# Spreading copies and norms between ScalarE, VectorE and GpSimd in a four-stage transformer block

## The chip, the cores and the metric

The kernel runs on one core of one Trainium2 chip. A core has five engines that run their own instruction streams and meet through semaphores: TensorE (PE in the profile, with its weight loads as PEld), VectorE (DVE), ScalarE (ACT), GpSimd (POOL) and SyncE (SP), which here only issues transfers. The metric is the device time of one execution in microseconds (us); shorter is better. The time of a kernel is the median of its runs.

## The reference

The input `x` is 8 batches of 128 tokens with 128 features, in float32. Eight sublayers are applied, each as `x = x + f(layernorm(x))`: four pairs of a cross attention over a context of 77 tokens and a feed-forward part. This change touches the third pair (called L2) and everything after it:

```python
x = x + _L1_ffn_ref(...)      # 64 experts, three per token: rows of y are gathered and weighed
x = x + _L2_xattn_ref(_layernorm(x), ctx, ...)   # rotary, 16 heads of 8, norms after, ReLU feed-forward
x = x + _L2_ffn_ref(_layernorm(x), ...)          # 6 local attention layers, window 32, 16 heads of 64
x = x + _L3_xattn_ref(_layernorm(x), ctx, ...)   # 8 heads of 64
x = x + _L3_ffn_ref(_layernorm(x), ...)          # 2 local attention layers, window 64, 8 heads of 64

# one local layer, h = features 64..127 taken from the token before
q, k, v = split(shift(x) @ Wqkv)
q, k = rotate(l2norm(q) * qs), rotate(l2norm(k) * ks)
x = x + local_attention(q, k, v) @ Wo
h = layernorm(shift(x)) * g + b
a, gate = split(h @ W1 + b1)
x = x + (a * gelu(gate)) @ W2 + b2
```

`_L2_xattn_ref` itself normalises twice: `x = layernorm(query + o)`, then `layernorm(x + relu(x @ W1) @ W2)`.

## The kernel before, in words

The activations stay on the chip: one batch is 128 partitions (tokens) by 128 features. Nearly all matmuls are in float32.

**How the order is made.** A layer doesn't issue instructions. It adds *steps* to a `Plan` (line 537): what a step reads and writes, and a nominal cost in ns on each engine that may run it, such as `{"ACT": 490, "DVE": 450}`. `arranged` (line 606) then plays the whole plan through with these costs: whenever an engine is free it takes the ready step of lowest rank, and a step with two engines goes to the one that comes to it first. The result is a fixed order per engine and a fixed choice of engine for each step. A changed cost, or a second engine for a step, can therefore reorder everything behind it, on PE too. There are two plans: "front" (up to the experts) and "later" (from L2's cross attention on). Once built, each engine runs its own list strictly in that order.

**The gather stage.** `plan_later` takes the batches two by two. For one batch, `one` (line 1586) has GpSimd issue three indirect transfers (`gathered`, line 1504) that fetch the rows of the experts' result; VectorE weighs and adds them to `x` (line 1517). Then comes the norm (`normed` and `scaled`, lines 772 and 778): VectorE finds mean and variance (lines 783, 785); GpSimd adds epsilon (776), takes the power -1/2 (790), negates the mean (791) and multiplies it by the root (792); ScalarE writes the normalised rows with that scale and bias (800), or VectorE does with mean and root alone (802). In this plan `norms_on_act` is set, so it is always ScalarE. The rows are transposed on PE (762), copied out of PSUM (749 on ScalarE, 751 on VectorE), projected twice, multiplied by the rotary tables (1549), and the two halves are added on GpSimd (1553). `attend_8` follows: scores (855), exponentials (863), sums and outputs (871), a reciprocal (877) and, only as a watch on overflow, two additions on GpSimd (881, 882). `layer` (line 1603) then takes two batches through norm, affine (1650), feed-forward with ReLU (1620 or 1622), and a second norm.

**The local layers.** They work on halves of four batches. `shifted` (line 1833) transposes `y` on PE and copies it out of PSUM as two pieces of 64 partitions, the second one token later. `queries_keys` (line 1851) does for each batch, for queries and keys and each group of eight heads: a projection (1847), squares on ScalarE (1868), two rotary products and a sum on VectorE (1869, 1871, 1873), an addition on GpSimd (1874), the inverse length (1899 to 1907), a product on GpSimd (1887), four transposes and a copy out of PSUM. `attention` follows (1952, 1958: band and scores; 1965: exponentials; 2013 and 2019, or 1992 and 1998: sums and outputs; 1973 to 1981: division; 1933: projection). `gated` (line 2028) is the feed-forward part; its step `gates` (2058, 2059) is one block on ScalarE: load the table for Gelu, three Gelus, load the table for exponentials back.

PE runs its matmuls in tile modes: whole, quarters, columns and so on; the plan charges a change of mode with 100 ns.

Of the kernel before, what the change touches and what calls it, by code (L numbers as in the profile page):

```python
# [19 lines left out]
ALU = mybir.AluOpType  # L20
# [4 lines left out]
P = 128  # L25
B = 8
KC = 77
EPS = 1e-5
# [676 lines left out]
class Work:  # L705
# [63 lines left out]
        self.plan.add({"PE": ns}, lambda e: nc.tensor.matmul(out(), lhsT=lhsT(), rhs=rhs(), start=start, stop=stop),  # L769
                      reads, writes, "full", opens)  # L770

    def normed(self, outs, ins, reads, writes, a=1.0, b=EPS, n=4):


        self.scaled(outs, ins, reads, writes,
                    lambda nc, t, v: nc.gpsimd.tensor_scalar(t, v, float(a), float(b), ALU.mult, ALU.add), n)

    def scaled(self, outs, ins, reads, writes, under, n=4):
        c, nc, plan = self.c, self.c.nc, self.plan
        st, mv, va, nb = self.tile([P, n, 6]), self.tile([P, n, 2]), self.tile([P, 2 * n]), self.tile([P, n])  # L780
        for k in range(n):
            one = reads if len(reads) != n else [reads[k]]
            plan.add({"DVE": 282}, lambda e, k=k: nc.vector.bn_stats(st()[:, k, :], ins(k)), one, [st])
        for k in range(n):
            plan.add({"DVE": 158}, lambda e, k=k: nc.vector.bn_aggr(mv()[:, k, :], st()[:, k, :]), [st], [mv])
        scale = lambda k: va()[:, n + k : n + k + 1]

        def root(e):
            under(nc, va()[:, 0:n], mv()[:, 0:n, 1])
            nc.gpsimd.tensor_tensor(va()[:, n : 2 * n], va()[:, 0:n], c.mhalf[:, 0:n], ALU.pow)  # L790
            nc.gpsimd.tensor_scalar(nb(), mv()[:, 0:n, 0], -1.0, None, ALU.mult)
            nc.gpsimd.tensor_tensor(nb(), nb(), va()[:, n : 2 * n], ALU.mult)

        plan.add({"POOL": 930 + 150 * n}, root, [mv], [va, nb])
        for k in range(n):
            one = reads if len(reads) != n else [reads[k]]

            def scaled(e, k=k):
                if e == "ACT":
                    nc.scalar.activation(outs(k), ins(k), AF.Identity, bias=nb()[:, k : k + 1], scale=scale(k))  # L800
                else:
                    nc.vector.tensor_scalar(outs(k), ins(k), mv()[:, k, 0:1], scale(k), ALU.subtract, ALU.mult)

            plan.add({"ACT": 490} if self.norms_on_act else {"ACT": 490, "DVE": 450}, scaled,
                     [*one, mv, va, nb], writes if len(writes) != n else [writes[k]])

    def softmax(self, sc, n, by_head=False):

# [29 lines left out]
    def attend_8(self, qT, at, kb, vz, j, wo, bias, mask=None, qv=None):  # L838
# [5 lines left out]
        c, nc, plan = self.c, self.c.nc, self.plan  # L844
# [21 lines left out]
        cl, rs, oT = self.tile([P, P]), self.tile([P, P]), self.tile([P, P])  # L866
# [11 lines left out]
        plan.add({"DVE": 282}, lambda e: nc.vector.tensor_tensor(oT(), av(), rs(), ALU.mult), [av, rs], [oT])  # L878

        def watch(e):  # L880
            nc.gpsimd.tensor_tensor(cl(), cl(), rs(), ALU.add)
            nc.gpsimd.tensor_tensor(c.total, c.total, cl(), ALU.add)

        plan.add({"POOL": 650}, watch, [rs, self.total], [cl, self.total])
        return self.projected_8(oT, wo, bias)

    def projected_8(self, oT, wo, bias):
# [359 lines left out]
class Routed:  # L1247
# [256 lines left out]
    def gathered(self, w, b):  # L1504

        c, nc, plan = w.c, w.c.nc, w.plan
        x = w.xs[b]
        for k in range(TOPK):
            g = w.tile([P, P])

            def get(e, k=k, g=g):
                self.got[b] = nc.gpsimd.indirect_dma_start(
                    out=g()[:, :], out_offset=None, in_=self.ys[:, :],
                    in_offset=bass.IndirectOffsetOnAxis(ap=self.srci[:, b, k : k + 1], axis=0)).ins

            plan.add({"POOL": 1000}, get, [w.landed], [g], tail=2300)
            plan.add({"DVE": 382}, lambda e, k=k, g=g: nc.vector.scalar_tensor_tensor(
                x(), g(), self.gate[:, b, k : k + 1], x(), ALU.mult, ALU.add), [g, x], [x])


class Context:
# [18 lines left out]
    def rotated(self, out, src, reads, name, which, m, n):  # L1540

        w = self.w
        c, nc, plan = w.c, w.c.nc, w.plan
        t = []
        for k, wname in enumerate((name, name + "_pair")):
            ps, tt = w.bank([P, m, n]), w.tile([P, m, n])
            w.mm(lambda ps=ps: ps().rearrange("p b s -> p (b s)"), lambda wname=wname: c.get("w", "L2_W" + wname), src,
                 reads, [ps], 1.7 * max(n * m, 130), opens=[tt])
            plan.add({"DVE": 200 + 1.1 * n * m}, lambda e, ps=ps, tt=tt, wname=wname, k=k: nc.vector.scalar_tensor_tensor(
                tt(), ps(), c.get("col", "L2_b" + wname), spread(self.rope[:, 2 * which + k, 0:n], m, 1), ALU.add, ALU.mult),  # L1550
                [ps], [tt])
            t.append(tt)
        plan.add({"POOL": 240 + 2.0 * n * m}, lambda e: nc.gpsimd.tensor_tensor(
            out() if m > 1 else out().unsqueeze(1), t[0](), t[1](), ALU.add), t, [out])

    def keys(self, h):
# [24 lines left out]
def plan_l2_xattn(w, ctx, route):  # L1581
# [4 lines left out]
    def one(b):  # L1586

        x, (xh, xT, qT, y) = w.xs[b], (w.tile([P, P]) for _ in range(4))
        route.gathered(w, b)
        w.normed(lambda k: xh(), lambda k: x(), [x], [xh], n=1)  # L1590
        tp = w.turn(lambda k: xh(), [xh], n=1)
        w.copy(xT, lambda: tp()[:, 0, :], [tp], [xT], 294, 290)
        ctx.rotated(qT, xT, [xT], "q", 0, 1, P)
        if b >= 4:
            ctx.values(b)
        out = w.attend_8(lambda: qT().unsqueeze(1), 0, ctx.kbs[b // 4], ctx.vzs[b % 4], b % 4, c.get("w", "L2_Wo"),
                         c.get("row", "L2_xattn_bo"), qv=qT)
        plan.add({"DVE": 282}, lambda e: nc.vector.tensor_tensor(y(), xh(), out(), ALU.add), [xh, out], [y])
        ys[b] = y
# [3 lines left out]
    def layer(b0, n):  # L1603
        xs, y = w.xs[b0 : b0 + n], [ys[b0 + j] for j in range(n)]
        y1 = w.tile([P, n, P])
        w.normed(lambda k, y1=y1: y1()[:, k, :], lambda k, y=y: y[k](), y, [y1], n=n)
        affine(w, y1, "L2_xattn_g1", "L2_xattn_b1", n)
        yT = w.tile([P, n, P])
        tp = w.turn(lambda k, y1=y1: y1()[:, k, :], [y1], n=n)
# [26 lines left out]
        plan.add({"DVE": 145 + 134 * n}, lambda e, y1=y1, y2=y2, out=out: nc.vector.tensor_tensor(y2(), y1(), out(), ALU.add),  # L1636
                 [y1, out], [y2])
        y3 = w.tile([P, n, P])
        w.normed(lambda k, y3=y3: y3()[:, k, :], lambda k, y2=y2: y2()[:, k, :], [y2], [y3], n=n)
        affine(w, y3, "L2_xattn_g2", "L2_xattn_b2", n)  # L1640
        xv = c.x[:, b0 : b0 + n, :]
        plan.add({"POOL": 80 + 300 * n}, lambda e, y3=y3, xv=xv: nc.gpsimd.tensor_tensor(xv, xv, y3(), ALU.add), [y3, *xs], xs)
# [115 lines left out]
class Local:  # L1758
# [74 lines left out]
    def shifted(self, b0, n):  # L1833

        nc, plan = self.c.nc, self.plan
        hs = self.tile([P, n, P])
        y = self.y
        tp = self.turn(lambda k: y[:, b0 + k, :], self.ys[b0 : b0 + n], n=n)
        plan.add({"POOL": 150}, lambda e: nc.gpsimd.memset(hs()[64:128, :, 0:1], 0.0), [], [hs])
        self.copy(lambda: hs()[0:64], lambda: tp()[0:64], [tp], [hs], 180 + 103 * n)  # L1840
        self.copy(lambda: hs()[64:128, :, 1:P], lambda: tp()[64:128, :, 0 : P - 1], [tp], [hs], 180 + 103 * n)
        return hs

    def projected(self, layer, hs, j, o, opens):
# [6 lines left out]
    def queries_keys(self, layer, hs, j):  # L1851
# [33 lines left out]
        for i in range(2 * ng):  # L1885
# [2 lines left out]
                t(), t1(), spread(r()[:, 8 * i : 8 * i + 8], 64, 2), ALU.mult), [t1, r], [t])  # L1888
            tp = self.turn(lambda k, t=t: t().rearrange("p h d -> p (h d)")[:, k * P : (k + 1) * P], [t])
            qT = self.tile([P, 4, P])  # L1890
            self.copy(qT, tp, [tp], [qT])
            out.append(qT)
        return out[:ng], out[ng:]

# [398 lines left out]
```

## Time and profile before

| what | value |
| --- | --- |
| median of three runs | 1497.15 us (1496.13 to 1500.06) |
| the profiled execution | 1488.41 us, its span 1486.4 us |
| PE busy, share of the span | 1389.6 us, 93% |
| VectorE, ScalarE, GpSimd busy | 918.6, 918.3, 825.9 us |
| mean granted TensorE clock | 0.977 of full speed |
| copies out of PSUM on ScalarE (749) | 519, mean 561 ns |
| copies out of PSUM on VectorE (751) | 73, mean 643 ns |

Times in a profile are those of one execution; it was 8.7 us shorter than the median. The span runs from the first to the last instruction. The stages by time: front and experts to about 374 us, gathers and L2's cross attention mixed with the first local layers to about 525 us, the six local layers of L2 to about 1200 us, L3 to the end. A busy PE in the profile is one with a matmul in flight; "idle before" is the time that an engine stood still just before an instruction.

### The profile page before, as it was taken

Reading aid. Unit: us, or ns where it says so; the run is one execution under the profiler, and the core shown is the slowest. Engines: PE = TensorE matmul, PEld = TensorE weight load, DVE = VectorE, ACT = ScalarE, POOL = GpSimd, SP = SyncE. Lnnn points to the kernel's source line nnn. Section 1 sums busy time; section 2 is a strip of 40 time slices with the busy share of each in tenths; the row PEclk is TensorE's granted clock in tenths of the full one; section 3 lists DMA queues with packets and bytes.
Section 4 is the critical chain, followed back from the end, with each engine's and each line's share of the span. In section 5 each row is a group of like instructions: output and inputs, shape, how many; then the busy total and the mean of one; then the engine's idle time right before and its main releaser. Section 6 shows DMA issues by size and latency. Waiting matters only on the chain.

```text
span 1486.4 us, 39191 instructions
## 1 busy us (share of the span) xinstructions
PE 1389.6 (93%) x15991; PEld 955.2 (64%) x15991; DVE 918.6 (62%) x1998; ACT 918.3 (62%) x1913; POOL 825.9 (56%) x1282
## 2 busy tenths in 40 slices
PE   8999997798889999999999999999999998889995
PEld 6776675565576666667566666756666666566654
DVE  7542676433459765685958668595866855658563
ACT  4665654343456675766667676666766675667663
POOL 5210235310788975765849586584948662628471
PEclk9999998799799999999999999999999999999997
DMA  9500001597501001000100100010000011000000
GB/s 321 175 1 1 9 5 54 184 337 263 190 13 72 2 2 58 17 2 2 58 17 2 45 31 2 2 58 16 2 2 23 11 65 40 23 2 2 1 9 11
DMA packets 44111, 79.07 MB, mean 53 GB/s; under 512 B 4582, under 2 KB 21542, under 8 KB 42768
## 3 DMA queue, kind: packets, MB, share of 16 engines
q1 hardware_dynamic: 38032, 71.21, 14.0%
q0 software_dynamic: 1536, 3.15, 0.7%
q8 instruction: 128, 2.10, 0.6%
q10 hardware_dynamic: 4352, 2.10, 0.5%
q14 instruction: 63, 0.52, 0.1%
HBM read 67.63 MB, written 8.81 MB: 51 GB/s over the span
## 4 chain that ended last, share of the span: by engine, by line
PE 39%; DVE 17%; POOL 12%; ACT 6%; issue 3%; DMA 2%; POOLq 0%; ACTq 0%; DVEq 0%; SPq 0%
PE mm L1847 7%; PE mm L762 6%; DVE big L1871 4%; DVE big L1869 4%; PE mm L1933 4%; DVE few L1873 4%; POOL big L1874 3%; PE mm L2074 3%; POOL big L1887 3%; PE mm L2019 3%; PE mm L1958 3%; PE mm L2051 3%; PE mm L2064 2%; POOL tiny L790 2%; DMA big<-in_experts_dram 1%
## 5 line engine op out<-in xcount | busy, mean ns | idle before, releaser
L749 ACT COPY big<-mm 128x512 f32<-128x512 f32 (+4 forms) x519 | 278.4, 561 | 220.9 <-PE mm L762 127.3
L1874 POOL TENSOR_TENSOR big<-big,big 128x512 f32<-128x512 f32 x224 | 284.2, 1276 | 225.5 <-DVE big L1871 218.1
L1847 PE MATMUL mm<-wide,big 128*128 128x512 f32 x672 | 317.0, 598 | 8.4 <-ACT big L749 8.4
L762 PE MATMUL mm<-ident,big 128*128 128x128 f32 (+1 forms) x1430 | 204.3, 279 | 26.8 <-DVE big L751 5.3
L1887 POOL TENSOR_TENSOR big<-big,few 128x512 f32<-128x512 f32 x224 | 227.2, 1043 | 1.6
L762 PEld LDWEIGHTS mm<-ident,big 128*128 128x128 f32 (+1 forms) x1430 | 161.4, 142 | 102.9 <-POOL big L1887 35.9
L1869 DVE TENSOR_TENSOR big<-mm,big 128x512 f32<-128x512 f32 x224 | 152.9, 683 | 56.7 <-ACT big L1868 56.2
L1847 PEld LDWEIGHTS mm<-wide,big 128*128 128x128 f32 x672 | 117.3, 191 | 103.6 <-issue 79.4
L1868 ACT ACTIVATE big<-mm 128x512 f32<-128x512 f32 x224 | 133.1, 597 | 77.3 <-PE mm L1847 70.3
L1871 DVE TENSOR_TENSOR big<-mm,big 128x512 f32<-128x512 f32 x224 | 152.7, 682 | 5.3 <-ACT big L1868 5.3
L1873 DVE TENSOR_REDUCE few<-big 128x8 f32<-128x512 f32 x224 | 151.4, 676 | 6.5 <-ACT big L1868 6.5
L1965 ACT ACTIVATE big<-mm 128x512 f32<-128x512 f32 x224 | 118.1, 610 | 28.0 <-PE mm L1958 27.4
L1933 PE MATMUL mm<-narrow,big 128*128 128x128 f32 x896 | 114.0, 279 | 3.7 <-DVE big L1981 3.7
L1933 PEld LDWEIGHTS mm<-narrow,big 128*128 128x128 f32 x896 | 105.6, 192 | 18.0 <-DVE big L1981 12.5
L1975 DVE TENSOR_TENSOR mm<-mm,big 128x512 f32<-128x512 f32 x64 | 44.6, 696 | 117.0 <-ACT big L1974 111.2
L2019 PEld LDWEIGHTS mm<-big,big 128*32 128x32 f32 x3072 | 85.9, 110 | 28.1 <-issue 27.4
L1958 PE MATMUL mm<-big,big 64*64 64x64 f32 (+2 forms) x3584 | 100.4, 238 | 1.1 <-ACT big L749 1.1
L1958 PEld LDWEIGHTS mm<-big,big 64*64 64x64 f32 x3584 | 94.2, 133 | 6.2 <-ACT big L749 2.0
L2019 PE MATMUL mm<-big,big 128*32 128x128 f32 x3072 | 92.8, 273 | 0.0
L1981 DVE SCALAR_TENSOR_TENSOR big<-mm,big 128x512 f32<-128x512 f32 x112 | 73.0, 687 | 5.6 <-PE mm L2019 0.6
L830 POOL TENSOR_TENSOR big<-big,tiny 128x308 f32<-128x308 f32 x40 | 28.5, 717 | 75.0 <-DVE tiny L827 34.2
L1471 DVE TENSOR_TENSOR big<-mm,p_col 128x512 f32<-128x512 f32 x32 | 20.7, 687 | 62.9 <-PE mm L762 53.0
(276 smaller groups left out, 2314.9 us busy)
## 6 DMA issues: line engine op xcount, KB each, us to landing
big<-in_experts_dram SPq DMA_DIRECT2D x128, 256.0 KB
wide<-in_l2a_dram SPq DMA_DIRECT2D x6, 1536.0 KB
narrow<-in_l2b_dram SPq DMA_DIRECT2D x6, 534.0 KB
narrow<-in_l2o_dram SPq DMA_DIRECT2D x6, 512.0 KB
kept<-big SPq DMA_DIRECT2D x16, 154.0 KB
big<-kept SPq DMA_DIRECT2D x16, 154.0 KB
p_w<-in_w_dram SPq DMA_DIRECT2D x1, 2048.0 KB
expert_rows<-big SPq DMA_DIRECT2D x8, 256.0 KB
```

The costliest lines, as they stand in the source:

```text
L749: nc.scalar.copy(out(), in_())
L762: nc.tensor.transpose(tp()[:, k, :], v(k), c.ident)
L1847: self.plan.add({"PE": 860}, lambda e: nc.tensor.matmul(ps(), lhsT=hs()[:, j, :], rhs=wqkv()[:, o : o + 512], start=True, stop=True), [hs, ...
L1868: yield lambda e: nc.scalar.activation(sq(), heads(), AF.Square)
L1869: yield lambda e: nc.vector.tensor_tensor(t1(), heads(), spread(rot()[:, 2 * kind, :], 8, 1), ALU.mult)
L1871: yield lambda e: nc.vector.tensor_tensor(halves(t2()), halves(heads())[:, :, ::-1, :], sin(), ALU.mult)
L1873: yield lambda e: nc.vector.tensor_reduce(ss()[:, lo : lo + 8], sq(), AX.X, ALU.add)
L1874: yield lambda e: nc.gpsimd.tensor_tensor(t1(), t1(), t2(), ALU.add)
L1887: plan.add({"POOL": 1062}, lambda e, t=t, t1=t1, i=i: nc.gpsimd.tensor_tensor(t(), t1(), spread(r()[:, 8 * i : 8 * i + 8], 64, 2), ALU.mul ...
L1933: nc.tensor.matmul(out(), lhsT=oT()[:, k, :], rhs=wo()[:, 4 * g + k, :], start=(g == 0 and k == 0), stop=(4 * g + k == nch - 1))
L1958: nc.tensor.matmul(sc[s]()[at : at + 64, k, q:end], lhsT=kT()[lo : lo + 64, k, at : at + 64], rhs=qT()[lo : lo + 64, k, q:end], start=Fals ...
L2019: nc.tensor.matmul(avs[half]()[32 * t : 32 * t + 32, k, :], lhsT=vs[t // 2]()[:, at : at + 32], rhs=prs[t]()[:, k, :], start=True, stop=True)
```

## The change

The steps keep what they compute. Some get a second engine, some another one, and some nominal costs are others.

- Norms with `on_dve=True` (the one behind the gathers and the two inside L2's cross attention) are written by VectorE only, and their GpSimd step leaves out the two instructions for the bias.
- The two copies of `shifted` and the copy of turned queries and keys may go to VectorE as well.
- The rotary addition and the watch may go to VectorE as well.
- The nominal cost of the watch on GpSimd goes from 650 to 920, that of a gather from 1000 to 1290.

```diff
-    def normed(self, outs, ins, reads, writes, a=1.0, b=EPS, n=4):
+    def normed(self, outs, ins, reads, writes, a=1.0, b=EPS, n=4, on_dve=False):
...
-            nc.gpsimd.tensor_scalar(nb(), mv()[:, 0:n, 0], -1.0, None, ALU.mult)
-            nc.gpsimd.tensor_tensor(nb(), nb(), va()[:, n : 2 * n], ALU.mult)
-
-        plan.add({"POOL": 930 + 150 * n}, root, [mv], [va, nb])
+            if not on_dve:
+                nc.gpsimd.tensor_scalar(nb(), mv()[:, 0:n, 0], -1.0, None, ALU.mult)
+                nc.gpsimd.tensor_tensor(nb(), nb(), va()[:, n : 2 * n], ALU.mult)
+
+        plan.add({"POOL": (500 if on_dve else 930) + 150 * n}, root, [mv], [va] if on_dve else [va, nb])
...
-            plan.add({"ACT": 490} if self.norms_on_act else {"ACT": 490, "DVE": 450}, scaled,
-                     [*one, mv, va, nb], writes if len(writes) != n else [writes[k]])
+            plan.add({"DVE": 450} if on_dve else {"ACT": 490} if self.norms_on_act else {"ACT": 490, "DVE": 450}, scaled,
+                     [*one, mv, va] if on_dve else [*one, mv, va, nb], writes if len(writes) != n else [writes[k]])
...
         def watch(e):
-            nc.gpsimd.tensor_tensor(cl(), cl(), rs(), ALU.add)
-            nc.gpsimd.tensor_tensor(c.total, c.total, cl(), ALU.add)
+            on = nc.gpsimd if e == "POOL" else nc.vector
+            on.tensor_tensor(cl(), cl(), rs(), ALU.add)
+            on.tensor_tensor(c.total, c.total, cl(), ALU.add)
 
-        plan.add({"POOL": 650}, watch, [rs, self.total], [cl, self.total])
+        plan.add({"POOL": 920, "DVE": 560}, watch, [rs, self.total], [cl, self.total])
...
-            plan.add({"POOL": 1000}, get, [w.landed], [g], tail=2300)
+            plan.add({"POOL": 1290}, get, [w.landed], [g], tail=2300)
...
-        plan.add({"POOL": 240 + 2.0 * n * m}, lambda e: nc.gpsimd.tensor_tensor(
+        plan.add({"POOL": 240 + 2.0 * n * m, "DVE": 145 + 1.1 * n * m}, lambda e: (nc.gpsimd if e == "POOL" else nc.vector).tensor_tensor(
             out() if m > 1 else out().unsqueeze(1), t[0](), t[1](), ALU.add), t, [out])
...
-        w.normed(lambda k: xh(), lambda k: x(), [x], [xh], n=1)
+        w.normed(lambda k: xh(), lambda k: x(), [x], [xh], n=1, on_dve=True)
...
-        w.normed(lambda k, y1=y1: y1()[:, k, :], lambda k, y=y: y[k](), y, [y1], n=n)
+        w.normed(lambda k, y1=y1: y1()[:, k, :], lambda k, y=y: y[k](), y, [y1], n=n, on_dve=True)
...
-        w.normed(lambda k, y3=y3: y3()[:, k, :], lambda k, y2=y2: y2()[:, k, :], [y2], [y3], n=n)
+        w.normed(lambda k, y3=y3: y3()[:, k, :], lambda k, y2=y2: y2()[:, k, :], [y2], [y3], n=n, on_dve=True)
...
-        self.copy(lambda: hs()[0:64], lambda: tp()[0:64], [tp], [hs], 180 + 103 * n)
-        self.copy(lambda: hs()[64:128, :, 1:P], lambda: tp()[64:128, :, 0 : P - 1], [tp], [hs], 180 + 103 * n)
+        self.copy(lambda: hs()[0:64], lambda: tp()[0:64], [tp], [hs], 180 + 103 * n, 145 + 134 * n)
+        self.copy(lambda: hs()[64:128, :, 1:P], lambda: tp()[64:128, :, 0 : P - 1], [tp], [hs], 180 + 103 * n, 145 + 134 * n)
...
-            self.copy(qT, tp, [tp], [qT])
+            self.copy(qT, tp, [tp], [qT], 591, 682)
```

More of the change, by code (lines that the diff above doesn't have):

```diff
@@ L770, in mm, with scaled @@
                       reads, writes, "full", opens)
-    def normed(self, outs, ins, reads, writes, a=1.0, b=EPS, n=4):
+    def normed(self, outs, ins, reads, writes, a=1.0, b=EPS, n=4, on_dve=False):
         self.scaled(outs, ins, reads, writes,
-                    lambda nc, t, v: nc.gpsimd.tensor_scalar(t, v, float(a), float(b), ALU.mult, ALU.add), n)
-    def scaled(self, outs, ins, reads, writes, under, n=4):
+                    lambda nc, t, v: nc.gpsimd.tensor_scalar(t, v, float(a), float(b), ALU.mult, ALU.add), n, on_dve)
+    def scaled(self, outs, ins, reads, writes, under, n=4, on_dve=False):
         c, nc, plan = self.c, self.c.nc, self.plan
```

## The prediction, made before the changed kernel ran

> **What bounds the kernel now.** I read the page's busy table and slices first, to see which engine is full and where. Rows: busy time and share; then tenths of 40 slices of 37 us.
>
> ```profile
> PE 1389.6 (93%) x15991; PEld 955.2 (64%) x15991; DVE 918.6 (62%) x1998; ACT 918.3 (62%) x1913; POOL 825.9 (56%) x1282
> ...
> PE   8999997798889999999999999999999998889995
> ...
> POOL 5210235310788975765849586584948662628471
> PEclk9999998799799999999999999999999999999997
> ```
>
> PE is full from slice 14 to slice 31. Before it (slices 10 to 12) GpSimd is the busiest engine while PE drops to 8 and its clock to 7 tenths. Behind it, in L3, PE drops to 8 again. So I cut the span into stretches (columns: stretch, then busy time of PE, PEld, DVE, ACT, POOL, the clock, DMA):
>
> ```profile
> 383.00:398.00 15.00, 10.39 (x134) 8.59 (x138) 6.91 (x21) 3.79 (x8) 12.38 (x24) 0.55 0.82 270
> 398.00:411.00 13.00, 10.56 (x197) 8.58 (x190) 8.84 (x33) 4.96 (x10) 10.18 (x20) 0.86 0.54 197
> 411.00:423.00 12.00, 11.12 (x140) 9.57 (x141) 5.60 (x17) 5.07 (x11) 10.46 (x20) 0.86 0.09 24
> ...
> 446.00:525.00 79.00, 76.66 (x934) 50.68 (x933) 60.23 (x124) 55.14 (x117) 72.62 (x111) 1.00 0.10 35
> 575.00:1200.00 625.00, 619.97 (x7699) 415.63 (x7694) 436.92 (x792) 422.14 (x812) 427.83 (x587) 1.00 0.06 21
> ```
>
> Three regimes. (1) Gathers, 374.5 to 423: the first gather is issued at 374.5, the last at 421.98. Weighted with the clock, PE does about 7.8 + 10.4 x 0.55 + 10.6 x 0.86 + 11.1 x 0.86 = 32 us of full-speed work in 48.5; GpSimd paces it. (2) Local layers of L2: PE stands still for 5 us in 625; nothing can be won there, only lost. (3) L3 from 1200: PE waits again. The waits of ScalarE in 385 to 425 (line, who it waited for, total, times, longest) and PE's in L3 name the two places:
>
> ```profile
> ACT row L800 <- POOL tiny L792: 10.5, 5, 4.2
> ...
> PE mm L1847 <- ACT big L749: 8.4, 3, 3.6
> ```
>
> [...] The trace has the 128x128 addition at 454 ns on GpSimd (1553) and about 285 ns on VectorE for its like (1598): 1.6 times. [...] here the weights of 1952 start 0.17 us late behind transposes.
>
> **The change part by part.** The order in which the changed program's instructions stand gives the counts; durations are from the trace of before.
>
> *a. GpSimd's list up to the last gather.* Before: 24 gathers, 7 roots of four instructions, 6 rotary additions, 4 watches, 2 affine steps. After: 24 gathers, 8 roots of two, 2 additions, 2 watches, 2 affine. The rows:
>
> ```profile
> L1512 POOL DMA_INDIRECT row<-expert_ys,srci x24 | 23.6, 982 | 7.2 <-issue 5.9 <-PE mm L892 0.5 <-DVE tiny L785 0.3
> L791 POOL TENSOR_SCALAR tiny<-tiny 128x4 f32<-128x4 f32 (+2 forms) x53 | 12.3, 232 | 0.0
> L792 POOL TENSOR_TENSOR tiny<-tiny,tiny 128x4 f32<-128x4 f32 (+2 forms) x53 | 10.6, 200 | 4.4
> L1553 POOL TENSOR_TENSOR row<-row,row 128x128 f32<-128x128 f32 x8 | 3.6, 454 | 0.1
> ```
>
> With 0.19 for 776, 0.65 for 790 (0.57 for one column, 0.72 for two) and 0.91 for a watch, before is 24 x 0.98 + 7 x 1.26 + 6 x 0.45 + 4 x 0.91 + 2 x 0.64 = 40.0 us; after is 23.5 + 8 x 0.84 + 2 x 0.45 + 2 x 0.91 + 1.3 = 34.2. Both carry the same 7.2 us of idle at the gathers. The list is 5.8 us shorter. The transfers move up with it: the last lands about as much earlier, and the large weight loads on SP that are tied to batch 1's gathers stay behind them. But GpSimd's first rotary addition now follows its eighth gather with one root less ahead of it, and will wait some 0.8 us for its batch. I take **-5**; bounds 0 and -7 (PE has 16 us of slack here, more than this).
>
> *b. VectorE in the same stretch.* It takes 10 scaled rows at 404 ns, 3 additions, 2 watches, 3 ReLUs, and gives up 3 copies; its list grows from 28.9 to 33.9 us. It was busy 23.6 of 48.5 and waited 16.2 us for gathered rows, which cover the 5 us: 0. Uncovered, it is +5. The hop to ScalarE goes, but its queue now waits for the roots, with residual additions and reciprocals behind: rival 1.
>
> *c. GpSimd after the last gather.* Nine more roots lose 0.42 us each, two additions go: 9 x 0.52 with the gaps + 0.9 = 5.6 us less. PE's idle time from 423 to 525 is 21.11 of 23 and 76.66 of 79 used, 4.2 in all, so bounds are 0 and -4.2. PE is nearly full and most waits there move to its own queue: **-1**.
>
> *d. Local layers of L2.* 39 copies of 128x512 in all leave ScalarE (about 0.59 us) for VectorE (0.69), 2 to 4 per half layer. VectorE is busy 437 of 625, ScalarE 422: room for 35 x 0.69 = 24 us. PE's queue of projections hides them: 0; uncovered: rival 2. PE's list has the same matmuls, but 336 changes of tile mode for 322. 14 x 0.15 = **+2.1**. A change isn't a row of its own: bounds 0.1 each (+1.4) and 0.5, the mean idle of the weight loads of 1952 (28.9 us, 55 times; +7).
>
> *e. L3.* At two places the shifted copies are first in a half layer behind `gates` on ScalarE (columns: start, duration):
>
> ```profile
> 1262.66 0.60 PE L762 MATMUL mm<-ident,y_res 128*128 128x128 f32 x4
> ...
> 1263.18 2.06 DVE L2066 SCALAR_TENSOR_TENSOR big<-mm,p_col,big 128x512 f32<-128x512 f32 x3 [5.61 <-ACT big L2058]
> 1264.31 1.28 ACT L2059 ACT_TABLE_LOAD   x1
> 1265.61 1.17 ACT L749 COPY big<-mm 64x512 f32<-64x512 f32 x2
> 1266.83 0.70 PE L1847 MATMUL mm<-wide,big 128*128 128x512 f32 x1 [3.56 <-ACT big L749]
> ```
>
> The transposes end at 1263.3, but ScalarE still loads its table; PE stands 3.56 us. The same happens at 1331.6 to 1335.1. In the changed order both copies stand on VectorE there, just ahead of the three 2066, where VectorE had been idle for 5.61 us. They would run 1263.35 to 1264.7 (two of at most 0.69), and PE would start at 1264.75: 2.1 us earlier, twice: **-4.2**. 2066 comes 1.4 us late, then the down projection (2074); PE now has four projections instead of two ahead of that (3.4 us), which cover it. The chain of waits runs through both places, so the upper bound is -4.2; the lower is 0, if the chain moves to GpSimd's 1874 and 1887 behind.
>
> *f. Front.* One division goes to VectorE, one group of transposes moves: 0, within 1 either way: from 281 to 323 the chain of waits there runs through the experts' weights (big<-in_experts_dram, 5 to 6 us each), which are not touched.
>
> Sum: -5 - 1 + 2.1 - 4.2 = -8.1 us. Against the profiled execution's 1488.4 that is 1480.3; its span is 2 us less. The median of the runs shown is 8.7 us above the profiled one, and I take the difference over as it is: **1489.0**.
>
> **The rivals.** *1, the relief is swallowed by VectorE's queue.* ScalarE waited 13.1 us for roots in 385 to 425; if VectorE stands for as long, its stretch is 23.6 + 5 busy, 10.1 of other waits that it had, and 13.1: 51.8 for 48.5, +3.3 in place of -5. With c at 0 and +2.1 - 4.2 that gives +1.2: 1498.4. It starts to eat the gain once those waits pass 4.8 us. For it: roots stay on GpSimd between gathers of 1.25 us. Against: other instructions were placed between statistics and scaling. *2, PE waits in the local layers.* Each moved copy is 0.10 longer and comes behind, on average, half of a 0.68 us VectorE instruction: 0.44 us late; where nothing hides it, 35 x 0.44 = +15.4: 1504.4. For it: VectorE is busy 23.7 of 25 us in some stretches (650 to 675, 975 to 1000), and PE has no slack. Against: PE waited only 1.8 us there for VectorE's product ahead of the scores. It decides from (8.1 + 4.5) / 35 = 0.36 us a copy. *3, PE's slack is regained further*: the clock stays up since PE no longer starves, -7 for a, -4 for c, with e and +1.4: -13.8, 1483.4. *4, nothing happens at the copies*: excluded, the order shows them moved.
>
> **How the numbers follow.** Forecast 0.55, rival 1 0.20, rival 2 0.15, rival 3 0.10. About 0.3% (4.5 us) is what a measurement of this kernel can tell from no change: below 1492.7 is faster, above 1501.6 slower. Forecast: 0.48 faster, 0.06 same, 0.01 slower; rival 1: 0.02, 0.17, 0.01; rival 2: 0.02 same, 0.13 slower; rival 3 faster. Sums: 0.60, 0.25, 0.15. The range 1481 to 1503 takes in rivals 1 and 3 and the mild half of rival 2; the forecast's own is 1484 to 1494.
>
> **What would show it.** a: last gather near 417 instead of 422, with clock above 0.6 from 383 to 398. b: VectorE's waits for 790 below 5 us. c: PE past 525 with some 6 us more done. d: waits of PE for 751 near 0, period of a half layer 65.0 to 65.3 us. e: PE's wait ahead of 1847 behind `gates` near 1.5 us, twice. Wrong would make it: half layers over 65.5 us, gathers that end as late as before, or an L3 as long as before.

## The result and the profile after

The changed kernel took 1488.32 us in the median of five runs (1485.73 to 1491.81), against 1497.15 before: a ratio of 0.9945, 95% interval [0.9927, 0.9964]. Measured again later, beside runs of the kernel before on the third of the chips used for the experiments (the record doesn't name the chip of the first measurement), it gave 0.9991 [0.9978, 1.0004]: no change that can be told from none. That second measurement belongs to the result and is taken up below. The profiled execution took 1485.73 us, its span 1483.5.

The busy table and the slices of the changed kernel (rows as in the page of before):

```profile
PE 1390.2 (94%) x15991; PEld 958.3 (65%) x15991; DVE 958.1 (65%) x2082; ACT 886.6 (60%) x1842; POOL 814.1 (55%) x1237
...
PE   8999997798899999999999999999999999899996
...
POOL 5210235310668967656848585674849572628461
PEclk9999998699889999999999999999999999999998
```

About 40 us of work have gone to VectorE, ScalarE has lost 32 and GpSimd 12. PE has the same work. In slices 10 and 11 (counted from 0), where the gathers are, GpSimd falls from 7 and 8 tenths to 6 and 6. Of PE's three slices at 8 in L3 (33 to 35) one is left. The same stretches as before the change:

```profile
383.00:398.00 15.00, 10.88 (x161) 8.69 (x165) 8.63 (x30) 4.36 (x10) 11.31 (x18) 0.77 0.83 270
398.00:411.00 13.00, 10.61 (x201) 8.69 (x197) 8.70 (x32) 2.57 (x6) 8.71 (x12) 0.76 0.53 202
411.00:423.00 12.00, 11.62 (x127) 9.30 (x120) 7.26 (x22) 4.59 (x10) 7.21 (x13) 0.55 0.10 24
446.00:525.00 79.00, 76.43 (x918) 51.69 (x917) 65.49 (x131) 50.58 (x104) 72.89 (x110) 1.00 0.07 27
575.00:1200.00 625.00, 612.79 (x7559) 411.68 (x7550) 444.11 (x804) 403.13 (x774) 422.80 (x583) 1.00 0.06 19
```

GpSimd is relieved, but the clock is 0.55 in 411 to 423 where it had been 0.86. Weighted with the clock, as in the prediction, PE was busy for 22.8 us in the first three stretches against 24.4 before. And in the local layers PE now stands still for 12 us of 625 where it had stood for 5.

The groups of GpSimd that lost instructions, and its gathers (count, busy, mean in ns, idle before):

```profile
L1514 POOL DMA_INDIRECT row<-expert_ys,srci x24 | 23.6, 984 | 6.7 <-issue 5.2 <-PE mm L872 0.3 <-DVE tiny L785 0.3
...
L792 POOL TENSOR_SCALAR tiny<-tiny 128x4 f32<-128x4 f32 (+2 forms) x37 | 8.8, 238 | 0.0
...
L793 POOL TENSOR_TENSOR tiny<-tiny,tiny 128x4 f32<-128x4 f32 (+2 forms) x37 | 7.4, 199 | 3.1
```

Lines of the changed kernel stand one or two higher: 1514 is 1512 of before, 792 and 793 are 791 and 792. Sixteen roots lost their two bias instructions (53 to 37 of each). In L3, the first of the two places behind `gates` (start, duration):

```profile
1266.89 0.60 PE L762 MATMUL mm<-ident,y_res 128*128 128x128 f32 x4
1267.53 1.39 DVE L751 COPY big<-mm 64x512 f32<-64x512 f32 x2 [5.73 <-PE mm L762]
1268.54 1.28 ACT L2061 ACT_TABLE_LOAD   x1
1268.95 2.06 DVE L2068 SCALAR_TENSOR_TENSOR big<-mm,p_col,big 128x512 f32<-128x512 f32 x3
...
1268.97 3.27 PE L1849 MATMUL mm<-wide,big 128*128 128x512 f32 x7 [1.48 <-DVE big L751]
```

Both copies run on VectorE without waiting for ScalarE's Gelus and table load, and PE's wait of 3.56 us is 1.48 us.

**A division of the span that can be compared.** The front and the experts' weights move the whole program by several us (the first gather was issued at 374.2 to 379.9 us in the first ten profiles, at 384.5 to 386.9 in the four of the third chip). So I divide at the first gather and at the first matmul of `gated` (2034 before, 2036 after), which stands once in each half layer and in the parts like it. A is from the first gather to the fourth of these, B from there to the twelfth (727.1 to 1245.8 us in the profile of before: nearly all of L2's local layers and the start of L3), C to the fifteenth (which takes in both places behind `gates` of L3), and the tail is from the end of the last addition to `x` (1799 or 1801) to the end of the span. The trace also records when the throttle granted PE half of its clock; the last two columns sum that time within A and within C. Times in us, of the profiled executions; the labels are those of the experiments below:

| kernel | A | B | C | tail | half clock in A | half clock in C |
| --- | --- | --- | --- | --- | --- | --- |
| before | 352.6 | 518.7 | 171.0 | 11.8 | 20.5 | 0 |
| before again (b0_same) | 353.5 | 518.7 | 173.2 | 11.8 | 20.5 | 6.8 |
| after | 352.2 | 523.7 | 166.4 | 9.2 | 23.9 | 0 |
| a_gather | 353.7 | 518.9 | 171.1 | 9.2 | 27.3 | 0 |
| n_no_qt | 351.8 | 518.8 | 168.9 | 9.2 | 23.9 | 3.4 |
| d_qt | 356.4 | 523.7 | 172.9 | 9.3 | 23.9 | 6.8 |
| e_hs_l3 | 354.7 | 519.1 | 168.9 | 11.9 | 23.9 | 3.4 |
| g_short | 347.6 | 518.8 | 177.7 | 9.2 | 13.7 | 17.1 |
| d_order | 356.7 | 525.0 | 174.2 | 9.2 | 23.9 | 10.2 |
| d_fixed | 356.2 | 521.7 | 178.3 | 11.7 | 23.9 | 17.1 |
| third chip: f_after | 356.5 | 523.9 | 168.1 | 9.3 | 20.5 | 3.4 |
| third chip: n_no_qt_2 | 360.4 | 518.8 | 167.3 | 9.1 | 34.1 | 0 |
| third chip: e_warm | 357.1 | 518.8 | 170.9 | 11.8 | 27.3 | 0 |
| third chip: best | 354.3 | 519.1 | 170.4 | 9.2 | 27.3 | 6.8 |

B repeats within 0.4 us where nothing in it is changed, so it carries small differences. A of before's order (which e_hs_l3 and e_warm keep there) is 352.6 to 354.7 us on the first chips and 357.1 on the third, and grows with the time at half clock, from 20.5 to 27.3 us; so does C among the kernels that keep PE's two waits there (e_warm, below). Single profiles of A and C are to be read with these columns. From before to after the terms are -0.3 (front), -0.4 (A), +5.0 (B), -4.6 (C) and -2.6 (from there to the end, all of it in the tail): -2.9, the difference of the two spans.

### The profile page after: what moved, and what is told of

It reads as the page before. It is cut to its first block, busy times and chain, and to the rows that moved or that the text cites. A ratio compares the mean times of both kernels' runs of the same rounds, so it can differ in the third digit from the quotient of the medians.

```text
span 1483.5 us, 39104 instructions
## 1 busy us (share of the span) xinstructions
PE 1390.2 (94%) x15991; PEld 958.3 (65%) x15991; DVE 958.1 (65%) x2082; ACT 886.6 (60%) x1842; POOL 814.1 (55%) x1237
## 4 chain that ended last, share of the span: by engine, by line
PE 42%; DVE 17%; POOL 11%; ACT 5%; issue 3%; DMA 2%; POOLq 0%; DVEq 0%; ACTq 0%; SPq 0%
PE mm L1849 7%; PE mm L762 6%; PE mm L1935 5%; POOL big L1876 4%; DVE big L1871 4%; POOL big L1889 4%; DVE big L1873 3%; DVE few L1875 3%; PE mm L2076 3%; PE mm L2053 3%; PE mm L2066 3%; PE mm L1960 2%; PE mm L2021 2%; PE mm L1463 2%; DVE big L1983 1%
## 5 line engine op out<-in xcount | busy, mean ns | idle before, releaser
L749 ACT COPY big<-mm 128x512 f32<-128x512 f32 (+2 forms) x475 | 254.1, 562 | 227.7 <-PE mm L762 116.6
L751 DVE COPY big<-mm 128x512 f32<-128x512 f32 (+5 forms) x117 | 74.4, 651 | 56.4 <-PE mm L762 36.0
```

What stands on the lines that cost most here:

```text
L749: nc.scalar.copy(out(), in_())
```

## The experiments

My theory was the prediction's sum: the gathers pay, L3 pays, the local layers cost little. The rivals: the relief is swallowed by VectorE's queue, or PE waits for the copies in the local layers. The experiments take the change apart. Each ratio is against the kernel before on the same chip.

**b0_same: the kernel before, unchanged.** 

> The kernel before, unchanged, run as if it were a change. Theory: the profiled execution that the prediction used (1488.4 us) was a short one, and the last gather, the first gated step (530.0 us) and the steps of 65.0 us per half layer come out as before within 0.5 us; the time is 1497 us and the ratio 1.000. Rival: the times differ by what the chip or the day gives, and ratios under 0.3% mean nothing.

1494.98 us, ratio 0.9999 [0.9986, 1.0011]. The same kernel's profile is 4.5 us longer in span than the one that I predicted from: 2.2 of them in C, 0.9 in A.

**d_qt: only the copy of turned queries and keys gets VectorE.**

```diff
-            self.copy(qT, tp, [tp], [qT])
+            self.copy(qT, tp, [tp], [qT], 591, 682)
```

> The kernel before with one edit: the copy of turned queries and keys may go to VectorE. Up to the experts and through the gathers the order stays as it was. Theory (from the two traces): the copies on VectorE break the even rhythm of the local layers; a pair of half layers takes 131.3 us for 130.0, from 335 changes of tile mode for 322 and from VectorE's division (1981) coming late to the projection: about +4 to +7 us, 1501 to 1504. The prediction's term: +2.1, 1499. Rival: the copies relieve ScalarE and the time falls below 1495.

1500.18 us, ratio 1.003 [1.002, 1.004]: this part alone makes the kernel slower. B is 5.0 us longer, as in the changed kernel.

**n_no_qt: the changed kernel without that copy's second engine.**

```diff
-            self.copy(qT, tp, [tp], [qT], 591, 682)
+            self.copy(qT, tp, [tp], [qT])
```

> The changed kernel with the copy of turned queries and keys back on ScalarE alone; all else as changed. Theory: the gain of the gathers and of L3's shifted copies stays, the loss in the local layers goes: half layers of 65.0 us again, 4 to 7 us below the changed kernel: 1481 to 1484. Rival: the gain comes from the copies, and the time goes back to 1492 or more.

1484.1 us, ratio 0.9909 [0.989, 0.9928]. B is back at 518.8. The changed kernel is better without one of its parts.

**a_gather: the changed kernel without either kind of copy**, so with the norms, the watch, the rotary addition and the costs of the gather stage alone (both `copy` calls as before). 

> The changed kernel with both kinds of copies of the local layers back on ScalarE: what is left are the norms on VectorE, the rotary additions, the watch and the new nominal costs. Theory: last gather at 419 for 422, the first gated step 4 to 5 us earlier, half layers of 65.0 us and L3 as before: -4 to -6 us, 1491 to 1493. Rival 1 of the prediction: VectorE's queue takes the relief back and the time is 1496 to 1498.

1491.92 us, ratio 0.9975 [0.9964, 0.9986], -3.8 us. But A is 353.7, as in b0_same on the same chip (353.5), if with more time at half clock. The tail is 2.6 us shorter, so by the medians 1.2 us are left for the gather stage, and the interval takes in none.

**g_short: what the relief of GpSimd is worth where the order stays.** Before's order on every engine; sixteen norms leave out the two bias instructions, and ScalarE gets a constant as bias. This leaves out the subtraction of the mean in those norms.

```diff
+            if not short:
-            nc.gpsimd.tensor_scalar(nb(), mv()[:, 0:n, 0], -1.0, None, ALU.mult)
-            nc.gpsimd.tensor_tensor(nb(), nb(), va()[:, n : 2 * n], ALU.mult)
+                nc.gpsimd.tensor_scalar(nb(), mv()[:, 0:n, 0], -1.0, None, ALU.mult)
+                nc.gpsimd.tensor_tensor(nb(), nb(), va()[:, n : 2 * n], ALU.mult)
...
-                    nc.scalar.activation(outs(k), ins(k), AF.Identity, bias=nb()[:, k : k + 1], scale=scale(k))
+                    nc.scalar.activation(outs(k), ins(k), AF.Identity, bias=(c.mhalf if short else nb())[:, k : k + 1], scale=scale(k))
```

> The kernel before in its own order on every engine, but the roots of the 16 norms of L2's cross attention leave out GpSimd's two instructions for the bias, and ScalarE takes a constant bias instead (so the mean is not taken off there: that part of the computation is left out). GpSimd's list up to 525 us is 16 x 0.42 = 6.7 us shorter, and nothing else changes. If GpSimd's list paces the gathers, as the prediction had it: -4 to -6 us at the first gated step and in the time. If the chain of each batch through PE, ScalarE and VectorE does (the traces of the changed kernels: PE idle 16.5 us from first gather to fourth gated step with or without the relief): -1 to -2 us.

1490.52 us, ratio 0.9951 [0.9934, 0.9969], -7.4 us, of which 2.6 are the tail: some 4.8 for the relief. A is 347.6, 5.0 us less than in the best A of before; in it PE stood 1.8 us less, and its busy time for the same work is 3.1 us less, with 13.7 us at half clock for 20.5. So the relief is real, and the changed kernel keeps little of it. Two places show where it goes. The first is GpSimd's waits over the gathers and the cross attention (line, who it waited for, total, times, longest), first g_short, then a_gather:

```profile
POOL tiny L776 <- DVE tiny L785: 4.5, 4, 3.1
```

```profile
POOL tiny L776 <- DVE tiny L785: 10.3, 6, 4.2
...
POOL row L883 <- DVE row L878: 2.5, 3, 1.1
...
POOL big L1652 <- DVE tiny L785: 1.0, 1, 1.0
```

GpSimd now stands longer in front of the roots, since VectorE finds mean and variance (785) later. In part that is VectorE's longer list: in a wait of 3.05 us in a_gather it does, among others, a watch that had been GpSimd's. In part it isn't: in the longest wait, 4.2 us, VectorE itself stood 2.8 us for PE.

The second is the new order behind the gathers. From the first gather to the first `gated` step and from there to the fourth (stretch, then busy time of PE, PEld, DVE, ACT, POOL, the clock, DMA), first before, then the changed kernel:

```profile
374.51:529.97 155.46, 142.60 (x1795) 100.40 (x1794) 97.79 (x248) 92.21 (x196) 134.31 (x235) 0.93 0.19 66
529.97:727.10 197.13, 193.52 (x2396) 130.46 (x2395) 137.04 (x248) 131.53 (x253) 130.49 (x181) 1.00 0.07 23
```

```profile
374.22:525.67 151.45, 140.82 (x1789) 101.06 (x1788) 112.33 (x290) 78.36 (x162) 122.66 (x191) 0.92 0.20 67
525.67:726.40 200.73, 194.94 (x2402) 130.96 (x2401) 139.60 (x251) 131.26 (x253) 131.91 (x183) 1.00 0.07 23
```

So the first `gated` step comes 4.0 us sooner after the first gather, with six matmuls fewer done, and 3.6 of these are gone at the fourth. In a_gather, without the copies, the second part takes 67.8 + 59.9 + 72.2 = 199.9 us, 59.9 + 72.2 + 65.0 = 197.1 before: PE's busy time is 1.0 us longer there, its standing 1.7. g_short differs from a_gather in two things, the order and the work that VectorE took over, and no run separates them. Nor do single profiles say how much is lost: of three pairs with the same time at half clock, the new order's A is 2.5 and 3.4 us shorter in two (after against e_hs_l3, a_gather against e_warm) and 3.9 longer in one (f_after against before).

**e_hs_l3: before, with the shifted copies free for VectorE in L3 alone.**

```diff
+        dve = 145 + 134 * n if self.name == "L3_ffn" else None
-        self.copy(lambda: hs()[0:64], lambda: tp()[0:64], [tp], [hs], 180 + 103 * n)
-        self.copy(lambda: hs()[64:128, :, 1:P], lambda: tp()[64:128, :, 0 : P - 1], [tp], [hs], 180 + 103 * n)
+        self.copy(lambda: hs()[0:64], lambda: tp()[0:64], [tp], [hs], 180 + 103 * n, dve)
+        self.copy(lambda: hs()[64:128, :, 1:P], lambda: tp()[64:128, :, 0 : P - 1], [tp], [hs], 180 + 103 * n, dve)
```

> The kernel before with one edit: the two copies of the shifted residual may go to VectorE in L3's local layers; they do in two half layers behind the Gelus, and all before 1240 us keeps its order. Prediction's term e: PE's wait ahead of the first projection goes from 3.56 to 1.5 us at both places: -4.2 us. The kernel without the query copies was 9.9 us below the one without both kinds of copies, so if that is all theirs: -9 to -10, of which 2.6 from a shorter end of the program. If the waits only move on in L3: 0.

1490.02 us, ratio 0.9949 [0.9934, 0.9965]: -7.9 us against the 1497.95 of before there (by the interval -5.2 to -9.9), where the two shortened waits are 4.2.

**d_order: the order of d_qt with every copy on ScalarE.** The plan is told of both engines, the instruction goes to ScalarE whatever it chose.

```diff
-            self.copy(qT, tp, [tp], [qT])
+            plan.add({"ACT": 591, "DVE": 682}, lambda e, qT=qT, tp=tp: nc.scalar.copy(qT(), tp()), [tp], [qT])
```

> PE's order of the kernel with the query copies on either engine (335 changes of tile mode), but all these copies are issued on ScalarE all the same. If the order of PE costs the time in the local layers: pairs of half layers stay at 131.3 us and the time at 1500. If VectorE's lateness costs it: back to 130.0 us a pair and 1495 to 1497. If ScalarE was rightly spared, the copies are now late on it and a pair is longer than 131.3.

**d_fixed: before's order, every sixth of these copies on VectorE**, unknown to the plan.

```diff
-            self.copy(qT, tp, [tp], [qT])
+            self.turned_copies = getattr(self, "turned_copies", 0) + 1
+            on_dve = self.turned_copies % 6 == 0
+            plan.add({"ACT": 591}, lambda e, qT=qT, tp=tp, on_dve=on_dve: nc.vector.tensor_copy(qT(), tp()) if on_dve
+                     else nc.scalar.copy(qT(), tp()), [tp], [qT])
```

> The kernel before with PE's order as it was (322 changes of tile mode), but every sixth copy of turned queries or keys is issued on VectorE, 37 in all. If the order of PE costs the time: half layers of 65.0 us, and the time of the kernel before, or 2.6 us less if the end of the program is the short one. If VectorE is late for these copies (the prediction's rival 2, 0.44 us each): 65.5 to 66.5 us a half layer and +4 to +15 us.

d_order took 1503.61 us, ratio 1.004 [1.0028, 1.0052]; d_fixed 1503.31, 1.003 [1.0014, 1.0045]. I had meant them to decide between order and engine, and both cost: B is 525.0 with the order alone and 521.7 with the engine alone, against 518.7. They don't add up, since the changed kernel with both has 523.7. Nor is d_order the order alone in full: its plan left no room on ScalarE for copies that it had given to VectorE. What the order does is read from PE's waits from the first to the eleventh `gated` step (652 to 659 us), first before, then d_order, then the changed kernel:

```profile
PE mm L762 <- ACT big L800: 2.5, 10, 0.5
PE mm L1952 <- DVE big L1871: 1.8, 9, 0.2
...
PE mm L1933 <- DVE big L1981: 0.7, 1, 0.7
```

```profile
PE mm L1933 <- DVE big L1981: 4.8, 9, 0.7
PE mm L762 <- ACT big L800: 3.4, 7, 0.5
PE mm L762 <- ACT big L1891: 2.0, 6, 0.3
```

```profile
PE mm L1935 <- DVE big L1983: 8.0, 15, 1.1
PE mm L762 <- DVE big L751: 2.2, 5, 0.4
PE mm L762 <- POOL big L1889: 0.9, 3, 0.4
```

In the new order PE comes to attention's output projection (1933, then 1935) before VectorE has divided (1981, then 1983), and to transposes whose bank hasn't been copied out (the copy 1891, late on ScalarE, in d_order; 751 in the changed kernel). All of PE's waits in this stretch sum to 6.7 us before, 12.7 in d_order and 12.6 after; PE's busy time is 645.2, 645.6 and 646.1.

**f_after and n_no_qt_2: the changed kernel and the one without the copies of turned queries, both on the third chip.**

> The changed kernel as it is, so that the versions below are compared with it on one chip: about -0.55% against before (ratio 0.9945), and again two half layers that take about 131.3 us together where before takes 130.0.

> The changed kernel without the copies of turned queries on VectorE, a second time, for more executions. If those copies are a loss, the ratio to before is 0.990 to 0.993 again and lies below that of the changed kernel beside it, with the ten half layers at about 654.8 us against 659. If the first measurement was the chip's mood, the two kernels agree within 0.3%.

Before took 1508.01 us there. f_after: 1506.56, ratio 0.9991 [0.9978, 1.0004], a miss: I had expected 0.9945. n_no_qt_2: 1498.48, ratio 0.9928 [0.9903, 0.9953]. So without these copies the kernel is 0.5% faster than with them on the same chip (1498.48 / 1506.56 = 0.9946), and the earlier measurements of these copies (d_qt, n_no_qt) are confirmed. B of f_after is 523.9 and n_no_qt_2's 518.8, as in the earlier profiles. On the third chip the first gather came 12.7 us later than in the first measurement, and then GpSimd stood longer for VectorE's statistics. Its waits from the first gather to the first `gated` step of f_after:

```profile
POOL tiny L776 <- DVE tiny L785: 12.9, 4, 10.3
```

Yet that isn't where the two measurements part. Before has no profile on this chip, but e_warm keeps its order through A: there A of f_after is 0.6 us the shorter (356.5 for 357.1), much as after's was (352.2 for 352.6). What differs is that f_after's first gather came 2.1 us later than e_warm's (after's 0.3 sooner than before's), and that from the fifteenth `gated` step to the last addition it takes 60.0 us, 10.2 of them at half clock, for e_warm's 57.9 with 6.8 (57.9 and 57.8 with 6.8 in before and after). These are 4.5 of the 7 us that the measurements lie apart, in single profiles; the rest I can't place.

**e_warm: does the length of PE's wait in L3 count for more than the time waited?** Before, with sixteen extra transposes of `y_res` at the two places, whose result is the same bank again.

```diff
-            self.hs[l, b0] = self.shifted(b0, n)
+            self.hs[l, b0] = self.shifted(b0, n, 5 if self.name == "L3_ffn" and l == 0 else 1)
...
-            for k in range(n):
+            for k in [*range(n)] * times:
```

> The kernel before, with its order and all its copies on ScalarE; only in the first two half layers of the third network's local layers TensorE repeats the four transposes of y_res four times more (16 extra transposes, 1.8 us, into the same bank), work that is thrown away. ScalarE is busy until after they end, so the copies start when they did: TensorE's wait there shrinks from 3.56 to about 1.8 us and not one instruction gets earlier. If only the length of the wait counted, the time is that of before or up to 1 us longer (ratio 1.000). If an idle stretch of 3.56 us lowers the granted clock in the work behind it, the two stretches behind the gates are at clock 1.00 (71.0 us for the first), and the median falls by 2 to 4 us (ratio 0.997 to 0.9985).

1503.04 us, ratio 0.997 [0.9955, 0.9986], -5.0 us, somewhat more than the 2 to 4 that the clock theory expected; the other one had expected no gain. One of the two places in e_warm, then the first place in g_short and in e_hs_l3:

```profile
1277.50 2.35 PE L762 MATMUL mm<-ident,y_res 128*128 128x128 f32 x20
1281.66 1.98 PE L1847 MATMUL mm<-wide,big 128*128 128x512 f32 x4 [1.82 <-ACT big L749]
```

```profile
1266.95 3.45 PE L1848 MATMUL mm<-wide,big 128*128 128x512 f32 x4 [3.56 <-ACT big L749]
```

```profile
1270.42 3.70 PE L1848 MATMUL mm<-wide,big 128*128 128x512 f32 x8 [1.48 <-DVE big L751]
```

In g_short four matmuls after a wait of 3.56 us take 3.45 us, 0.86 each; in e_warm, after 1.82 us, four take 1.98, and in e_hs_l3, after 1.48 us, eight take 3.70: 0.5 and 0.46 each. In the profile of before the wait of 3.56 us cost nothing more: four took 1.98. The stretches from the twelfth `gated` step to the thirteenth and from there to the fourteenth have these clocks (the column after GpSimd's count), first of g_short, then of e_warm:

```profile
1242.80:1318.20 75.40, 66.63 (x634) 46.02 (x635) 45.46 (x110) 45.60 (x114) 36.09 (x61) 0.93 0.04 12
1318.20:1382.80 64.60, 58.72 (x453) 36.75 (x451) 43.13 (x87) 40.74 (x82) 40.81 (x66) 0.95 0.01 1
```

```profile
1260.70:1331.60 70.90, 63.63 (x650) 44.15 (x651) 45.39 (x110) 45.39 (x114) 36.05 (x61) 1.00 0.04 13
1331.60:1393.90 62.30, 58.06 (x469) 36.64 (x467) 42.93 (x87) 41.01 (x82) 40.81 (x66) 1.00 0.00 1
```

Cut to about the end of the waits at the two places and the time right behind, they are, first g_short, then e_warm:

```profile
1267.40:1270.70 3.30, 3.30 (x7) 1.52 (x6) 1.34 (x3) 0.86 (x2) 0.00 (x0) 0.50 0.00 0
1335.70:1342.40 6.70, 5.78 (x15) 3.71 (x16) 3.04 (x6) 2.05 (x4) 1.27 (x1) 0.50 0.00 0
```

```profile
1281.60:1285.00 3.40, 3.34 (x18) 2.38 (x19) 1.55 (x3) 1.20 (x3) 0.11 (x1) 1.00 0.00 0
1349.40:1356.20 6.80, 6.22 (x33) 4.31 (x34) 4.29 (x8) 2.31 (x4) 2.55 (x2) 1.00 0.01 2
```

The same holds for all fourteen profiles. Seven keep the waits of about 3.56 us: at 10 of their 14 places the clock is halved from about the wait's end on, for 3.4 or 6.8 us, and at the four of before and a_gather it isn't. Seven have them shortened to 1.82 or 1.48 us: at none of these 14 places is it halved. In the seven that keep the waits, C goes with the time at half clock: 171.0 and 171.1 us with none, 172.9 and 173.2 with 6.8, 174.2 with 10.2, 177.7 and 178.3 with 17.1.

What decides between the 10 places where the clock is halved behind a wait of 3.56 us and the four where it isn't was not shown. Nor is one long wait needed: about 4 us behind the twelfth `gated` step the clock is halved in six of the fourteen profiles (for 6.8 us in g_short), where PE's longest waits from 3 us ahead of that step on are 0.38, 0.74 and 0.75 us, the same in all. So the sixteen useless transposes make the kernel faster (ratio 0.997), and the clock behind the two places is what they change: 1.00 in e_warm's two short stretches, 0.50 in g_short's.

**best: the relief in before's order, with L3's copies.** The two bias instructions of the sixteen norms become one on VectorE, put out with the ScalarE instruction that needs it, unknown to the plan; beside it the edit of e_hs_l3.

```diff
+                    if short and k == 0:
+                        nc.vector.scalar_tensor_tensor(nb(), mv()[:, 0:n, 0], -1.0, va()[:, n : 2 * n], ALU.mult, ALU.mult)
                     nc.scalar.activation(outs(k), ins(k), AF.Identity, bias=nb()[:, k : k + 1], scale=scale(k))
```

> Before's order, with the third network's shifted copies free to go to VectorE, and with the roots behind the gathers short on GpSimd: the two instructions for the bias become one on VectorE, put out just ahead of the ScalarE instruction that needs it and unknown to the planner. If the relief of GpSimd is worth its 5 to 6 us where the order stays (as in the run that left the mean out) and the third network's copies their 7.6, the sum is -12 to -15 us, some 1483 us (ratio 0.990 to 0.992), ahead of the changed kernel. If the instruction that waits on VectorE for GpSimd's root holds up the queue behind it, as the first rival says, the first gated step is late again (155 us after the first gather in place of 150.5) and the gain is that of the third network alone (ratio 0.995).

1497.28 us against 1508.01 of before there: ratio 0.9917 [0.9897, 0.9938], -10.7 us, the top of the first expectation's ratio and short of its 12 us. On this chip it beats both kernels (1497.28 / 1506.56 = 0.9938 of the changed one); n_no_qt_2 is 1.2 us behind it, which is no difference. A is 354.3 against e_warm's 357.1, both with 27.3 us at half clock: 2.8 us of relief here, not 5, with the first gather 10 us later than where g_short was measured. The medians don't show even that: -10.7 less e_hs_l3's -7.9 and the tail's -2.6 leaves 0.2, with two or three us of doubt in each.

## Why the prediction was right or wrong

The number held (1489.0 predicted, 1488.3 measured), but by errors that cancelled, which was luck, and in the second measurement the same kernel is within 0.3% of before. By the prediction's own steps:

- **a, GpSimd's list: the count was right, the gain was not.** From the first gather to the end of the last one GpSimd was busy 34.0 us for 34.2 predicted. The last gather came at 419.21 in place of 421.98, not 417. At a fixed order the relief is worth some 5 us (g_short), with c's 1 inside it. In the changed kernel A fell by 0.4 for the -6 of a and c: 4.0 had come by the first `gated` step, and 3.6 went again up to the fourth. The step that failed is that the new order of the first half layers was put at nothing, with VectorE's added work (b).
- **b, "cover the 5 us: 0".** Half right. VectorE's waits for roots in 385 to 425 were 0.8 us, so rival 1's stall (13.1) didn't come. But the mirror image did: GpSimd's roots wait for VectorE's statistics, 7.9 us over the stage in after, 10.3 in a_gather and 12.9 in f_after, for 4.1 before. I asked who is queued behind the root on VectorE, and not who waits for what VectorE does next. Rival 1's outcome was nearly right for A and its place wrong; and since 4.0 us did reach the first `gated` step, these waits are not most of the loss.
- **d, the local layers: "0; uncovered: rival 2", and +2.1 for mode changes.** The step that failed: PE's queue didn't hide the moved copies and the new order. B is +5.0, in profiles from two chips. PE's busy time grew by 0.9 us for the 2.1 that I gave to mode changes. The 0.15 us each was an estimate from idle time of the weight loads: those of 1952 stood 0.17 us behind transposes in the trace of before, where PE itself stood for 0.00. Its waits grew by 5.9 us: those for the division ahead of the output projection by 7.3, with others going. Rival 2 had the sign, with three times the size (+15.4), but also only part of the cause: the new order, without one copy moved, does it too.
- **e, L3.** The mechanism as told, line for line: 3.56 to 1.48 us, and between profiles without half clock C falls from 171.0 to 166.4. The term was mis-sized: -7.9 us alone (e_hs_l3) for -4.2. It left out that the clock is halved behind 10 of the 14 waits of that length at these places, so a wait kept can cost more than its time (C of before is 171.0 us without half clock and, in b0_same, 173.2 with 6.8 us of it); e_warm takes 5.0 us off by halving the waits with nothing gained besides.
- **From profile to median: "I take the difference over as it is".** It wasn't constant. Before's profiled execution was 8.7 us better than its median, after's 2.6 better than its own. Both had C at the full clock, but behind waits of 3.56 us, which only before has, it was halved at 10 of 14 places, behind the shortened ones at none of 14, which fits. The two profiles differ by 2.7 us, the medians by 8.8. A sum made on that profile could see of e only the wait itself. That the conversion came out right is owed to the cancelling.
- **Not in the sum: the tail**, -2.6 us.

Rival 3 (clock stays up in the gathers) fell: 0.55 in 411 to 423, for 0.86 before. Of the signs that I had named as contrary, one came, half layers over 65.5 us (alternating 64.7 and 66.6, so 65.65), and one by half: the gathers ended 2.8 us sooner, not 5. The chances, 0.60 to 0.25 for faster over no change, fit what the two measurements gave.

From single parts, the medians add up as -3.8 (a_gather, 1491.92 - 1495.68) + 4.5 (d_qt, 1500.18 - 1495.68) - 7.9 (e_hs_l3) = -7.2 us, in which the tail's 2.6 stands twice: -4.6 with it once. Six shifted copies moved, four in L3 and two at the start of L2's local layers; those two have no run of their own. The two measurements of the whole are -8.8 and -1.5.

## What to carry to other kernels

Where a planner orders the work, a second engine for a step changes the order of everything behind it, so the worth of a moved instruction has to be tested at a fixed order as well as in the new one; here the relief was worth some 5 us in the old order (one run), and in the new one, where VectorE also had more work, little or nothing that lasts. On a full TensorE, add an engine to a step only where TensorE is seen to wait for that step (L3's two places), and not where the wait is already hidden (39 copies for +5 us). Look for long waits ahead of matmuls, such as the 3.56 us here, and read the granted clock right behind them (0.50 in g_short, 1.00 in e_warm): shortening the two here by 1.74 us each, with work that is thrown away, took 5.0 us off the median.

## What the runs showed of the hardware that I had not expected

- **Useless work that pays.** Sixteen extra transposes at each of two places took 5.0 us (0.3%) off the median, and the granted clock behind them stayed at 1.00.
- **The clock can fall without a long wait.** In six of fourteen profiles it was halved for 3.4 or 6.8 us where the longest wait close ahead was 0.75 us. Why it falls in six and not in eight wasn't tried.
- **The tail.** From the end of the last addition to the end of the span it is 11.7 to 11.9 us in five profiles and 9.1 to 9.3 in nine, and goes by the kernel: the three that were profiled twice kept their value. The last addition of the changed kernel, in a span of 1483.5 us:

```profile
1473.58 0.72 POOL L1801 TENSOR_TENSOR x_res<-x_res,y_res 128x256 f32<-128x256 f32 x1 [3.67 <-DVE y_res L2080]
```

  1483.5 - 1474.3 = 9.2. The cause is open: g_short differs from before by 32 fewer GpSimd instructions and one operand, has the same order, and lost 2.6 us there. It wasn't tried further.
- **Mode changes look cheap here.** Some thirteen more of them in the local layers came with 0.4 to 0.9 us more of PE's busy time: at most 0.07 us each, unless part of their cost lies in the waits that the profile puts down to other engines.
